# Two layers over an adjacency on one core: wo loaded by heads on SyncE, two weight rings, stores moved to SyncE and ScalarE, and the digits of a quarter of wq and wk made first and copied on chip

## The chip, the core and the metric

The kernel runs on one core of one Trainium2 chip. The time is the device time of one execution in microseconds (us). The kernel before was run three times: 2391.94, 2392.21 and 2393.85 us, median 2392.21 us.

## The reference

There are 64 graphs (batch entries) of 256 nodes with 512 features, x of shape 64 x 256 x 512 in float32, and one 0/1 matrix adj of 256 x 256 that all share. Layer 0 is masked attention with 8 heads of 64 columns, layer 1 multiplies by adj and by a weight; each adds its input and normalizes over the features.

```
q, k, v = x @ Wq + bq, x @ Wk + bk, x @ Wv + bv            # 8 heads of 64
scores  = q . k / 8 + (1 - adj) * -1e9
out     = softmax(scores) . v
x = layernorm(x + out @ Wo + bo)
x = layernorm(x + (adj @ x) @ weight + bias)
```

## The kernel before

The batch is worked in 32 pairs p (0 to 31) of two entries, so the four 128-row chunks of a pair make a moving operand of 512 columns.

**Digits.** A float32 product is made of three products of float32r operands. `split_high` (ScalarE, line 118), `split_rest` (VectorE, lines 123 and 124) and `split_scale` (ScalarE, line 127) cut a weight into the tiles high, low and diff; `x_high` and `x_rest` (lines 285, 289, 290) do it for x, `qk_high`, `qk_rest` and `k_low` (lines 378, 385 to 389, 394) for q and k. `product` (line 347) then issues 12 matmuls of 128 x 512 on line 339: three digits times four chunks k of the contraction, in the order low, high, diff of the second operand, or, for a few products marked `soon`, high first. Without digits a product takes four float32 matmuls.

**Weights.** The weights are cut once, in the first pairs, and each of the three digit tiles (1 MB) is kept in DRAM (`keep`, line 129, issued by GpSimd). From then on each stage loads its three tiles again (`load_w`, line 105, GpSimd). A stage is one of v, qk1 (heads 4 to 7 of q and k), o, qk0 (heads 0 to 3) and l; `STAGES` is their order, and a pool of six tiles `wr` holds the stage at work and the next one. `end_stage` starts the load of the stage after the next.

**Order.** PE, DVE (VectorE), ACT (ScalarE) and POOL (GpSimd) run in the order in which the program issues (`manual_schedule`); the queue of SP (SyncE), which loads and stores, is ordered by the framework. Each engine is in order: an instruction that waits holds all behind it.[...]

**The start.** `start` (line 696) writes the order of the first pair out by hand. Of q and k it multiplies the columns of heads 0 to 3 first: blocks (q, 0, 0), (k, 0, 0), (q, 0, 1), (k, 0, 1), each 128 columns of wq or wk, as float32, since no weight digits exist yet. Meanwhile DVE cuts x of pair 0 and then the weights of qk1 and v. Then follow `adj_t` (transposes of adj), `scores(0, 0)`, the blocks (q, 0, 2) to (k, 0, 3) and (v, 0, 0) to (v, 0, 3) with digits, `values(0, 0)` and `scores(0, 1)`. The digits of qk0, all 256 columns of wq and of wk, are cut in four steps (`ring_high`, `ring_rest`, `ring_scale` for k of 0 to 3) between v of pair 0 and `scores(0, 1)`; their first use is pair 1. `load_o` loads wo in four GpSimd DMAs, after which `bv_wo` multiplies bv by it.

**PSUM.** `banks` is a pool of eight banks. A score step takes eight at once, so the last score tiles wait until the tiles eight allocations earlier are copied out by ACT: in `values` those are zc (line 413) and vc (line 425).

**The end.** The last rows are normalized in two halves, one on ACT, one on DVE; ACT stores one (line 545), SP the other. A last check of the number range (line 782) lets every engine skip the general kernel behind it.

Of the kernel before, what the change touches and what calls it, by code (L numbers as in the profile page):

```python
# [15 lines left out]
P = 128  # L16
# [19 lines left out]
def fast(tc, x, adj, wq, bq, wk, bk, wv, bv, wo, bo, w1, b1, out):  # L36
# [34 lines left out]
    RAW, SCRATCH, W, UNCUT, BEGUN = {}, {}, {}, {}, {}  # L71

# [26 lines left out]
    STAGES += [("o", NP - 1), ("l", NP - 1)]  # L99
    ended = [0]  # L100

    def ring(name):
        return [wring.tile([P, 2, 2, D], F32R, name="wr") for _ in range(3)]

    def load_w(stage):
        name, p = stage
        if stage not in W and not (p in (0, NP - 1) and name in "ol"):
            W[stage] = ring(name)
            for i in range(3):
                nc.gpsimd.dma_start(W[stage][i], SCRATCH[name, i])  # L110

# [17 lines left out]
    def keep(name, i, part):  # L129

        SCRATCH[name, i] = scratch.tile([P, 2, 2, D], F32, name=f"{name}{i}")
        nc.gpsimd.dma_start(SCRATCH[name, i], part.bitcast(F32))

    def in_ring(f, name, p, k):

        stage = name, p
        if stage not in W:
            W[stage] = ring(name)
# [7 lines left out]
        if k == DC - 1 and f is not split_high:  # L146
            for i in (0, 2) if f is split_rest else (1,):
                keep(name, i, W[stage][i])

# [5 lines left out]

    def ring_scale(name, p, k):
        in_ring(split_scale, name, p, k)

# [38 lines left out]
    for i in range(4):  # L197
        load_x(1, i)
    bo_s, b1_s = on_all(bo, "bo"), on_all(b1, "b1")

    def small_ones():
# [6 lines left out]
    def load_o(k):  # L208
        if k % 2 == 0:
            RAW["o"] = two.tile([P, 2, D], F32, name="hl")  # L210
        RAW["o", k] = RAW["o"][:, k % 2]
        nc.gpsimd.dma_start(RAW["o", k], wo[k // 2 * HF:(k // 2 + 1) * HF].rearrange("(h a i) e -> a h i e", h=4, a=2)[k % 2])

    def load_l():
        t = two.tile([P, DC, D], F32, name="r")
# [58 lines left out]
    def x_t(p, k):  # L274
        if p < NP:
            XF[p, k] = two.tile([P, D], F32, name="xT")
            nc.vector.transpose(XF[p, k], XC.pop((p, k)))
            if p > 1 or k > 1:
                load_x(p + k // 2, (k + 2) % DC)

    def x_high(p, k):
# [32 lines left out]
    def operands(name, p, j, k):  # L314

        cols = slice(j * P, (j + 1) * P)
        if name == "v":
            pairs = [(XP[p, k][i][:, cols], W["v", p][i][:, k // 2, k % 2]) for i in range(3)]
        elif name in "qk":
            g, c = divmod(j, 2)  # L320
            if p == 0 and g == 0:
                return [(RAW[name][:, k, cols], XF[p, k])]
            e = slice(c * P, (c + 1) * P)
            w = [t[:, "qk".index(name)].rearrange("p s (k e) -> p (s k) e", k=2)[:, k, e] for t in W[f"qk{g}", p]]
# [6 lines left out]
        soon = p == 1 and name in "qk" and j == 0 or p == NP - 1 and name in "ol"  # L331
        return [pairs[i] for i in ((0, 1, 2) if soon else (1, 0, 2))]

    def parts_of(pm, name, p, j, of=(0, 3)):
# [12 lines left out]
    def product(name, p, j):  # L347
        if (name, p, j) in BEGUN:
            pm = BEGUN.pop((name, p, j))
            n = parts_of(pm, name, p, j, (1, 3))  # L350
        else:
            pm = banks.tile([P, D], F32, name="ps")
            n = parts_of(pm, name, p, j)
        scale = RHO if n == 3 else 1.0
        b, c = divmod(j, 2)
        if name in "ol":
            r = R[p][b][:, c]
            if c == 0:
                ST[p, name, b] = two.tile([P, 2], F32, name="sums")
            nc.vector.scalar_tensor_tensor(r, pm, scale, r, op0=OP.mult, op1=OP.add, accum_out=ST[p, name, b][:, c:c + 1])  # L360
        elif name == "v":
            if c == 0:
                V[p, b] = two.tile([P, NC, D], F32, name="v")
            nc.scalar.activation(V[p, b][:, c], pm, AF.Copy, scale=scale)
        else:
            T, bias = (K, bk_s) if name == "k" else (Q, bq_s)
            if c == 0:
                T[p, b] = one.tile([P, 2, 3, D], F32R if n == 3 else F32, name=name + "T")
            if n == 3:
# [326 lines left out]
    def start():  # L696
        make_identity(nc, ident)
        do(*((x_first, i) for i in range(4)), (biases,), *((x_high, 0, i) for i in range(4)), (small_ones,))
        qk1, v = (steps_of(*stage) for stage in STAGES[:2])
        high, rest, scale = ([(f, "qk0", 1, k) for k in range(DC)] for f in (ring_high, ring_rest, ring_scale))  # L700
        do((block, "q", 0, 0), (x_rest, 0, 0), (x_rest, 0, 1), qk1[0], (block, "k", 0, 0), (x_rest, 0, 2), (x_rest, 0, 3),
           qk1[1], (block, "q", 0, 1), qk1[2], v[0], (block, "k", 0, 1), v[1][:1], (x_t, 1, 0),
           (adj_t,), qk1[3])
        scores(0, 0)
        do(v[1][1:], (x_t, 1, 1), masks(0, 0, 0), (block, "q", 0, 2), v[2], *((load_o, k) for k in range(DC)), (qk_high, "q", 0, 2), (qk_rest, "q", 0, 2), v[3], (test_adj,),
           (block, "k", 0, 2), (x_high, 1, 0), (x_high, 1, 1), (qk_high, "k", 0, 2), (qk_rest, "k", 0, 2), masks(0, 0, 1),
           (block, "q", 0, 3), (k_low, 0, 2), (qk_high, "q", 0, 3), (qk_rest, "q", 0, 3), (x_rest, 1, 0), (x_t, 1, 2),
           (block, "k", 0, 3), (stage_end, 0), (qk_high, "k", 0, 3), (qk_rest, "k", 0, 3), (x_rest, 1, 1), (x_t, 1, 3), high[:2],
           (block, "v", 0, 0), (x_high, 1, 2), high[2:], (k_low, 0, 3), (block, "v", 0, 1), (x_rest, 1, 2),
           (block, "v", 0, 2), (x_high, 1, 3), (x_rest, 1, 3), (block, "v", 0, 3), (stage_end, 0), (load_r, 0), (load_l,))  # L710
        values(0, 0)
        scores(0, 1)
        do((bv_wo,), rest[:2], scale[:1], rest[2:3], scale[1:2], rest[3:], scale[2:])
        qk0 = [(f, name, 1, j) for j in range(2) for name in "qk" for f in (qk_high, qk_rest)]
        m = masks(0, 1, 0) + masks(0, 1, 1)
        do((begun, "q", 1, 0), (begun, "k", 1, 0), (block, "q", 1, 0), m[:4], qk0[:2], (block, "k", 1, 0), m[4:5], qk0[2:4], m[5:],
# [44 lines left out]
           (last_variance,), (root, 1), (less, p, "l", 1, c1), (normed, p, "l", 3, D // 2))  # L761

    PE, DVE, ACT, POOL = mybir.EngineType.PE, mybir.EngineType.DVE, mybir.EngineType.Activation, mybir.EngineType.Pool
    with tc.manual_schedule(engines={PE, DVE, ACT, POOL}):
        start()
        first(1, steps_of("o", 0))
# [2 lines left out]
        for w in range(2, NP - 1):  # L769
            first(w)  # L770
            second(w)
        ending()

    good = one.tile([P, 2, N // 32], F32, name="z")
# [186 lines left out]
```

## Time and profile before

| | |
|---|---|
| three runs, median | 2392.21 us (2391.94 to 2393.85) |
| the profiled execution | 2391.06 us, of which the span of the trace is 2389.2 us |
| PE busy | 2374.3 us, 99% of the span |
| DVE, ACT, POOL busy | 1991.0, 1505.4, 443.5 us |
| TensorE clock granted | 0.999 |
| DMA | 608.70 MB, 255 GB/s mean |

The sums below are made on the profiled span of 2389.2 us; the profiled execution took 1.9 us more than its span, and the median of the runs is 1.15 us above the profiled execution. In the profile's rows "idle before" is the idle time of the engine, and the arrow names what ended it. A DMA's "us to landing" runs from its issue on the queue to the arrival of its last byte.

### The profile page before, as it was taken

The numbers are of one execution on the slowest core, as the hardware profiler recorded it, in microseconds if no ns is written. First come the engines' busy times: TensorE is split into PE (matmuls) and PEld (weight loads), VectorE is DVE, ScalarE is ACT, GpSimd is POOL, SyncE is SP. The second block draws the span as 40 slices with busy tenths as digits, with TensorE's granted clock in tenths as the row PEclk, the third lists the DMA queues.
The fourth block names the chain that finished last, engine by engine and source line by source line (L and its number), as shares of the span: only waits on it lengthen the run. The fifth ranks groups of instructions, "written<-read, shape, count | busy, mean of one in ns | idle before, by whom it ended". The sixth has DMA issues, their size and how long they took to land.

```text
span 2389.2 us, 43002 instructions
## 1 busy us (share of the span) xinstructions
PE 2374.3 (99%) x16925; PEld 1907.5 (80%) x16925; DVE 1991.0 (83%) x3311; ACT 1505.4 (63%) x2793; POOL 443.5 (19%) x755
## 2 busy tenths in 40 slices
PE   9999999999999999999999999999999999999998
PEld 6788887888878888878888788887888878888776
DVE  7988888888888888888988888888888888888867
ACT  6666666566565665666656656666566665666655
POOL 1222111111111111121111112111111111121121
PEclk9999999999999999999999999999999999999999
DMA  9897788777888777887777967788778887777782
GB/s 295 274 310 244 265 255 283 259 230 256 260 265 271 241 237 256 264 293 238 236 255 254 310 240 224 265 255 286 258 227 261 261 264 268 238 244 255 256 274 62
DMA packets 373651, 608.70 MB, mean 255 GB/s; under 512 B 272316, under 2 KB 275908, under 8 KB 313156
## 3 DMA queue, kind: packets, MB, share of 16 engines
q0 software_dynamic: 71632, 500.21, 57.5%
q1 hardware_dynamic: 301104, 105.29, 20.4%
q8 instruction: 135, 2.21, 0.4%
q14 instruction: 72, 0.59, 0.1%
q10 hardware_dynamic: 708, 0.40, 0.1%
HBM read 551.29 MB, written 49.28 MB: 251 GB/s over the span
## 4 chain that ended last, share of the span: by engine, by line
PE 96%; DVE 1%; ACT 0%; issue 0%; POOLq 0%; ACTq 0%
PE ps L339 72%; PE ps L421 9%; PE ps L455 8%; PE ps L615 5%; PE ps L411 3%; DVE e L476 0%; DVE wr L124 0%; DVE wr L123 0%; PE ps L565 0%; DVE kT L389 0%; DVE qT L387 0%; DVE qT L385 0%; ACT kT L394 0%; DVE kT L385 0%; ACT waste L517 0%
## 5 line engine op out<-in xcount | busy, mean ns | idle before, releaser
L373 ACT ACTIVATE uncut<-ps,numbers 128x512 f32<-128x512 f32 x252 | 174.0, 690 | 274.0 <-PE ps L339 218.1
L476 DVE TENSOR_TENSOR e<-e,adjT 128x1024 f32<-128x1024 f32 x252 | 299.3, 1219 | 0.2 <-ACT e L470 0.2
L339 PE MATMUL ps<-low,wr 128*128 128x512 f32 x992 | 271.6, 395 | 0.0
L339 PE MATMUL ps<-wr,sl 128*128 128x512 f32 x1008 | 270.6, 390 | 0.1
L339 PE MATMUL ps<-wr,sh 128*128 128x512 f32 x1008 | 269.8, 389 | 0.0
L339 PE MATMUL ps<-wr,sd 128*128 128x512 f32 x1008 | 269.4, 389 | 0.0
L339 PE MATMUL ps<-high,wr 128*128 128x512 f32 x992 | 266.4, 390 | 0.0
L339 PE MATMUL ps<-diff,wr 128*128 128x512 f32 x992 | 265.0, 389 | 0.0
L523 POOL TENSOR_TENSOR ln<-ln,numbers 128x2 f32<-128x2 f32 x127 | 140.4, 1105 | 667.0 <-DVE ln L522 621.3
L470 ACT ACTIVATE e<-ps 128x512 f32<-128x512 f32 x504 | 253.3, 629 | 8.6 <-PE ps L455 8.6
L517 ACT ACTIVATE waste<-r,ln 128x512 bf16<-128x512 f32 x255 | 184.0, 722 | 104.6 <-DVE ln L510 98.9
L421 PE MATMUL ps<-e,v 128*32 128x256 f32 x4032 | 229.1, 379 | 0.0
L538 ACT ACTIVATE r<-r,ln 128x512 f32<-128x512 f32 x254 | 193.7, 811 | 55.1 <-DMA x<-in_x_dram 29.9
L339 PEld LDWEIGHTS ps<-wr,sh 128*128 128x128 f32 x1008 | 189.3, 188 | 39.9
L339 PEld LDWEIGHTS ps<-wr,sd 128*128 128x128 f32 x1008 | 189.2, 188 | 39.5 <-DMA wr<-o 0.2
L339 PEld LDWEIGHTS ps<-high,wr 128*128 128x128 f32 x992 | 186.2, 188 | 41.9 <-ACT e L470 0.8
L339 PEld LDWEIGHTS ps<-diff,wr 128*128 128x128 f32 x992 | 186.2, 188 | 39.1
L339 PEld LDWEIGHTS ps<-wr,sl 128*128 128x128 f32 x1008 | 186.9, 188 | 38.2 <-issue 0.4
L455 PEld LDWEIGHTS ps<-qT,kT 64*128 64x128 f32 x3056 | 187.8, 187 | 27.1 <-PE ps L421 12.4
L385 DVE SCALAR_TENSOR_TENSOR qT<-qT,uncut 128x512 fp32r<-128x512 f32 x126 | 86.8, 689 | 146.9 <-ACT qT L378 146.8
L339 PEld LDWEIGHTS ps<-low,wr 128*128 128x128 f32 x992 | 177.7, 188 | 35.5 <-ACT wr L127 0.6
L455 PE MATMUL ps<-qT,kT 64*128 64x256 f32 x3056 | 201.6, 285 | 0.5 <-ACT kT L394 0.5
(166 smaller groups left out, 4156.1 us busy)
## 6 DMA issues: line engine op xcount, KB each, us to landing
wr<-qk POOLq DMA_DIRECT2D x183, 1024.0 KB, 7.6
wr<-v POOLq DMA_DIRECT2D x93, 1024.0 KB, 6.8
wr<-o POOLq DMA_DIRECT2D x90, 1024.0 KB, 7.8
wr<-l POOLq DMA_DIRECT2D x90, 1024.0 KB, 8.6
r<-in_x_dram SPq DMA_DIRECT2D x32, 1024.0 KB, 12.0
out_dram<-r SPq DMA_DIRECT2D x62, 512.0 KB, 2.9
x<-in_x_dram SPq DMA_DIRECT2D x488, 64.0 KB, 5.4
qk<-wr POOLq DMA_DIRECT2D x6, 1024.0 KB, 8.3
```

Source lines behind the costliest of these rows:

```text
L339: nc.tensor.matmul(pm, *pairs[k][i], start=i == 0 and k == 0, stop=i == n - 1 and k == DC - 1)
L373: nc.scalar.activation(to, pm, AF.Identity, bias=bias[:, j:j + 1], scale=scale)
L385: nc.vector.scalar_tensor_tensor(low, high.bitcast(F32), -RHO, UNCUT.pop((name, p, j)), op0=OP.mult, op1=OP.add)
L411: nc.tensor.matmul(at[h * 32:(h + 1) * 32, b, :], ones, chunk[h], start=i == 0, stop=i == len(sm) - 1)
L421: nc.tensor.matmul(at[h * 32:(h + 1) * 32, a, :], V[p, b][:, kc, col:col + 32], E[p, g, b, kc][0][h % 2][:, h // 2, :], start=kc == 0, sto ...
L455: nc.tensor.matmul(sc[s][:, a, :], K[p, g][r, a, i, keys], Q[p, g][r, a, i, b * N:(b + 1) * N], start=i == digits[0], stop=i == digits[-1])
L470: nc.scalar.activation(e[s], sc[s], AF.Exp, scale=(RHO if (p, g) != (0, 0) else 1.0) * qscale)
L476: nc.vector.tensor_tensor(e, e, mask[:, kc:kc + 1, :].to_broadcast([P, e.shape[1], N]), op=OP.mult)
L517: nc.scalar.activation(waste, R[p][b][:, c], AF.Square, bias=t[0][:, c:c + 1], accum_out=t[1][:, c:c + 1])
L523: nc.gpsimd.tensor_tensor(t[2], t[1], power[:, cs], op=OP.pow)
L538: nc.scalar.activation(r[:, :cut], r[:, :cut], AF.Identity, scale=scale, bias=bias)
L615: nc.tensor.matmul(pm[:, j, :], t[:, i, mc, j * P:(j + 1) * P], adjT[:, mc, :], start=mc == 0 and i == 0, stop=mc == NC - 1 and i == 1)
```

## The change

- **Two rings.** The pool of six weight tiles becomes two pools of three, `wa` and `wb`, taken in turn by a stage's place in `STAGES`. The stage (v, 1) does not load its tiles again: it uses those of (v, 0), still in `wb`.
- **wo by heads.** Eight SP DMAs of 128 KB, four for each half of wo, in place of four GpSimd DMAs of 256 KB; they stand in SP's queue between the x loads of chunks 0, 1 and of chunks 2, 3 of pair 1.
- **Stores.** The digits of o and l are kept by SP instead of GpSimd. At the end both halves of the last rows are stored by ACT, and SP runs in program order as well.
- **The quarter.** The digits of the second 128 columns of wq and wk are cut first (`cut_high`, `cut_rest`, `cut_scale`), into tiles borrowed from the pools of low, diff, zc and vc. The blocks (q, 0, 1) and (k, 0, 1) use them: 12 matmuls each in place of four float32 ones. `cut_over` later copies them into the ring of (qk0, 1) by six SP DMAs of 256 KB; the first 128 columns are cut in place, in two steps each in place of four.
- The loads of x chunks 0 and 1 of pair 2 are issued after `cut_over`, before the loads of r and of the weight of layer 1.

```diff
-    wring = pool("wr", 6)
+    wrings = pool("wa", 3), pool("wb", 3)
...
+        if stage == ("v", 1):
+
+            W[stage] = W["v", 0]
+        elif stage not in W and not (p in (0, NP - 1) and name in "ol"):
+            W[stage] = ring(stage)
...
-        nc.gpsimd.dma_start(SCRATCH[name, i], part.bitcast(F32))
+        (nc.sync if name in "ol" else nc.gpsimd).dma_start(SCRATCH[name, i], part.bitcast(F32))
...
+        elif name == "qk0":
+
+            t = [w[:, k].rearrange("p s (k e) -> p (s k) e", k=2)[:, :, :P] for w in W[stage]]
+            f(RAW["qk"[k]][:, :, :P], t)
...
+    def cut(f, k):
+        if (k, 0) not in EARLY:
+            for i in range(3):
+                pool_of, name = ((four, "low"), (four, "diff"), (one, "zc"), (two, "vc"))[k + (2 if i == 2 else 0)]
+                EARLY[k, i] = pool_of.tile([P, DC, P], F32R, name=name)
+        f(RAW["qk"[k]][:, :, P:2 * P], [EARLY[k, i] for i in range(3)])
...
+    def cut_over():
+        W["qk0", 1] = ring(("qk0", 1))
+        for i, t in enumerate(W["qk0", 1]):
+            for k in range(2):
+                to = t[:, k].rearrange("p s (k e) -> p (s k) e", k=2)[:, :, P:2 * P]
+                nc.sync.dma_start(to.bitcast(F32), EARLY[k, i].bitcast(F32))
...
+        for h in range(4):
+            nc.sync.dma_start(t[h * 32:(h + 1) * 32], wo[g * HF + h * HD:g * HF + (h + 1) * HD].rearrange("(a i) e -> i a e", a=2))
...
-            if p == 0 and g == 0:
+            if p == 0 and j == 0:
                 return [(RAW[name][:, k, cols], XF[p, k])]
             e = slice(c * P, (c + 1) * P)
...
+            if p == 0 and g == 0:
+                w = [EARLY["qk".index(name), i][:, k] for i in range(3)]
...
-                    for queue, part in (nc.scalar, slice(0, cut)), (nc.sync, slice(cut, D)):
-                        if 0 < cut < D or part == slice(0, D):
-                            (queue if cut < D else nc.sync).dma_start(outr[p, b, :, c, part], r[:, part])
+                    for part in [slice(0, cut), slice(cut, D)] if 0 < cut < D else [slice(0, D)]:
+                        (nc.scalar if 0 < cut < D else nc.sync).dma_start(outr[p, b, :, c, part], r[:, part])
...
+        do((cut_high, 0), (cut_high, 1), (block, "q", 0, 0), (x_rest, 0, 0), (x_rest, 0, 1), (x_rest, 0, 2), (cut_rest, 0), (x_rest, 0, 3),
+           (cut_rest, 1), h, (cut_scale, 0), (block, "k", 0, 0), (cut_scale, 1), r[:2],
+           (block, "q", 0, 1), c[:2], r[2:], (block, "k", 0, 1), v[0], v[1][:1], (adj_t,), c[2:])
...
-           (block, "k", 0, 3), (stage_end, 0), (qk_high, "k", 0, 3), (qk_rest, "k", 0, 3), (x_rest, 1, 1), (x_t, 1, 3), high[:2],
+           (block, "k", 0, 3), (stage_end, 0), (cut_over,), (qk_high, "k", 0, 3), (qk_rest, "k", 0, 3), (x_rest, 1, 1), (x_t, 1, 3),
...
-        values(0, 0)
+        values(0, 0, (high[:1], high[1:]))
         scores(0, 1)
-        do((bv_wo,), rest[:2], scale[:1], rest[2:3], scale[1:2], rest[3:], scale[2:])
+        do(rest, scale, (bv_wo,))
```

From pair 1's scores to the end of the last pair but one, PE, DVE and ACT execute the same instructions in the same order in both kernels (two neighbours on DVE change places at the end).

More of the change, by code (lines that the diff above doesn't have):

```diff
@@ L70, in fast @@
     XC, XF, XP, R, Q, K, V, E, SM, O, SET, HL, ST, LN = ({} for _ in range(14))
-    RAW, SCRATCH, W, UNCUT, BEGUN = {}, {}, {}, {}, {}
+    RAW, SCRATCH, W, UNCUT, BEGUN, EARLY = {}, {}, {}, {}, {}, {}
     def load_x(p, i):
@@ L100, in fast, with ring @@
     ended = [0]
-    def ring(name):
-        return [wring.tile([P, 2, 2, D], F32R, name="wr") for _ in range(3)]
+    def ring(stage):
+        i = STAGES.index(stage) % 2
+        return [wrings[i].tile([P, 2, 2, D], F32R, name="w" + "ab"[i]) for _ in range(3)]
     def load_w(stage):
         name, p = stage
-        if stage not in W and not (p in (0, NP - 1) and name in "ol"):
-            W[stage] = ring(name)
+        if stage == ("v", 1):
+            W[stage] = W["v", 0]
+        elif stage not in W and not (p in (0, NP - 1) and name in "ol"):
+            W[stage] = ring(stage)
             for i in range(3):
@@ L137, in in_ring @@
         if stage not in W:
-            W[stage] = ring(name)
+            W[stage] = ring(stage)
         t = [w[:, k // 2, k % 2] for w in W[stage]]
@@ L145, in in_ring @@
             f(raw, [u.rearrange("p (k e) -> p k e", k=2) for u in t])
-        if k == DC - 1 and f is not split_high:
+        if k == (1 if name == "qk0" else DC - 1) and f is not split_high:
             for i in (0, 2) if f is split_rest else (1,):
@@ L157, in ring_scale, with cut_high, cut_rest, cut_scale @@
         in_ring(split_scale, name, p, k)
+    def cut(f, k):
[4 more added lines that the diff above has]
+        f(RAW["qk"[k]][:, :, P:2 * P], [EARLY[k, i] for i in range(3)])
+    def cut_high(k):
+        cut(split_high, k)
+    def cut_rest(k):
+        cut(split_rest, k)
+    def cut_scale(k):
+        cut(split_scale, k)
+    def cut_over():
[4 more added lines that the diff above has]
+                nc.sync.dma_start(to.bitcast(F32), EARLY[k, i].bitcast(F32))
     ones = cpool.tile([P, 32], F32, name="ones")
@@ L196, in fast @@
         nc.sync.dma_start(RAW["v", k], wv[k * P:(k + 1) * P])
-    for i in range(4):
+    for i in range(2):
+        load_x(1, i)
+    for g in range(2):
+        t = two.tile([P, 2, D], F32, name="hl")
+        for h in range(4):
+            nc.sync.dma_start(t[h * 32:(h + 1) * 32], wo[g * HF + h * HD:g * HF + (h + 1) * HD].rearrange("(a i) e -> i a e", a=2))
+        for a in range(2):
+            RAW["o", 2 * g + a] = t[:, a]
+    for i in range(2, 4):
         load_x(1, i)
@@ L206, in small_ones @@
             nc.gpsimd.memset(first_of_32[d * 32:d * 32 + 1], 1.0)
[L208 to L212, printed above, removed]
     def load_l():
@@ L277, in x_t @@
             nc.vector.transpose(XF[p, k], XC.pop((p, k)))
-            if p > 1 or k > 1:
+            if p > 1:
                 load_x(p + k // 2, (k + 2) % DC)
@@ L320, in operands @@
             g, c = divmod(j, 2)
-            if p == 0 and g == 0:
+            if p == 0 and j == 0:
                 return [(RAW[name][:, k, cols], XF[p, k])]
             e = slice(c * P, (c + 1) * P)
-            w = [t[:, "qk".index(name)].rearrange("p s (k e) -> p (s k) e", k=2)[:, k, e] for t in W[f"qk{g}", p]]
+            if p == 0 and g == 0:
+                w = [EARLY["qk".index(name), i][:, k] for i in range(3)]
+            else:
+                w = [t[:, "qk".index(name)].rearrange("p s (k e) -> p (s k) e", k=2)[:, k, e] for t in W[f"qk{g}", p]]
             pairs = [(w[i], XP[p, k][i]) for i in range(3)]
@@ L329, in operands @@
             pairs = [(t[i][:, k % 2, c * P:(c + 1) * P], W[name, min(p, NP - 2)][i][:, k // 2, k % 2]) for i in range(3)]
-        soon = p == 1 and name in "qk" and j == 0 or p == NP - 1 and name in "ol"
+        soon = name in "qk" and (p, j) in ((0, 1), (1, 0)) or p == NP - 1 and name in "ol"
         return [pairs[i] for i in ((0, 1, 2) if soon else (1, 0, 2))]
@@ L366, in product @@
             T, bias = (K, bk_s) if name == "k" else (Q, bq_s)
+            digits = (p, b) != (0, 0)
             if c == 0:
-                T[p, b] = one.tile([P, 2, 3, D], F32R if n == 3 else F32, name=name + "T")
-            if n == 3:
+                T[p, b] = one.tile([P, 2, 3, D], F32R if digits else F32, name=name + "T")
+            if digits:
                 to = UNCUT[name, p, j] = two.tile([P, D], F32, name="uncut")
@@ L698, in start @@
         do(*((x_first, i) for i in range(4)), (biases,), *((x_high, 0, i) for i in range(4)), (small_ones,))
[L699 to L703, printed above, removed]
+        h, r, c = ([(f, "qk1", 0, k) for k in range(DC)] for f in (ring_high, ring_rest, ring_scale))
@@ L704, in start @@
+        v = steps_of("v", 0)
+        high, rest, scale = ([(f, "qk0", 1, k) for k in range(2)] for f in (ring_high, ring_rest, ring_scale))
+        do((cut_high, 0), (cut_high, 1), (block, "q", 0, 0), (x_rest, 0, 0), (x_rest, 0, 1), (x_rest, 0, 2), (cut_rest, 0), (x_rest, 0, 3),
+           (cut_rest, 1), h, (cut_scale, 0), (block, "k", 0, 0), (cut_scale, 1), r[:2],
+           (block, "q", 0, 1), c[:2], r[2:], (block, "k", 0, 1), v[0], v[1][:1], (adj_t,), c[2:])
         scores(0, 0)
-        do(v[1][1:], (x_t, 1, 1), masks(0, 0, 0), (block, "q", 0, 2), v[2], *((load_o, k) for k in range(DC)), (qk_high, "q", 0, 2), (qk_rest, "q", 0, 2), v[3], (test_adj,),
+        do(v[1][1:2], masks(0, 0, 0), (x_t, 1, 0), v[1][2:], (x_t, 1, 1), (block, "q", 0, 2), v[2], (qk_high, "q", 0, 2), (qk_rest, "q", 0, 2), v[3], (test_adj,),
@@ L706, in start @@
            (block, "k", 0, 2), (x_high, 1, 0), (x_high, 1, 1), (qk_high, "k", 0, 2), (qk_rest, "k", 0, 2), masks(0, 0, 1),
            (block, "q", 0, 3), (k_low, 0, 2), (qk_high, "q", 0, 3), (qk_rest, "q", 0, 3), (x_rest, 1, 0), (x_t, 1, 2),
-           (block, "k", 0, 3), (stage_end, 0), (qk_high, "k", 0, 3), (qk_rest, "k", 0, 3), (x_rest, 1, 1), (x_t, 1, 3), high[:2],
-           (block, "v", 0, 0), (x_high, 1, 2), high[2:], (k_low, 0, 3), (block, "v", 0, 1), (x_rest, 1, 2),
-           (block, "v", 0, 2), (x_high, 1, 3), (x_rest, 1, 3), (block, "v", 0, 3), (stage_end, 0), (load_r, 0), (load_l,))
@@ L711, in start @@
-        values(0, 0)
+           (block, "k", 0, 3), (stage_end, 0), (cut_over,), (qk_high, "k", 0, 3), (qk_rest, "k", 0, 3), (x_rest, 1, 1), (x_t, 1, 3),
+           (block, "v", 0, 0), (x_high, 1, 2), (k_low, 0, 3), (block, "v", 0, 1), (x_rest, 1, 2),
+           (block, "v", 0, 2), (x_high, 1, 3), (x_rest, 1, 3), (block, "v", 0, 3), (stage_end, 0), (load_x, 2, 0), (load_x, 2, 1), (load_r, 0), (load_l,))
+        values(0, 0, (high[:1], high[1:]))
         scores(0, 1)
-        do((bv_wo,), rest[:2], scale[:1], rest[2:3], scale[1:2], rest[3:], scale[2:])
+        do(rest, scale, (bv_wo,))
@@ L763, in fast @@
     PE, DVE, ACT, POOL = mybir.EngineType.PE, mybir.EngineType.DVE, mybir.EngineType.Activation, mybir.EngineType.Pool
+    SP = mybir.EngineType.SP
     with tc.manual_schedule(engines={PE, DVE, ACT, POOL}):
@@ L771, in fast @@
             second(w)
+    with tc.manual_schedule(engines={PE, DVE, ACT, POOL, SP}):
         ending()
```

## The prediction

> **What bounds the kernel now.** I read the page first (PE busy 99%), then the table of stretches, to see where PE is not busy:
>
> ```profile
> 0.00:10.00 10.00, 5.65 (x22) 4.01 (x23) 2.70 (x7) 4.41 (x10) 1.20 (x13) 1.00 0.80 255
> 10.00:75.00 65.00, 64.54 (x441) 44.65 (x440) 59.44 (x86) 44.31 (x81) 11.53 (x21) 1.00 1.03 307
> 75.00:2300.00 2225.00, 2225.00 (x15917) 1795.06 (x15914) 1872.38 (x3088) 1407.24 (x2610) 414.68 (x698) 1.00 0.79 258
> 2300.00:2389.00 89.00, 79.12 (x555) 63.83 (x553) 56.52 (x133) 49.40 (x94) 16.05 (x23) 0.97 0.46 139
> ```
>
> After the stretch come its length, the busy time of PE, weight loads, DVE, ACT and POOL, the clock, the DMA share and GB/s. From 75 to 2300 us PE has no gap, and there the change leaves the order of PE, DVE and ACT as it is. So only what PE does up to about 75 us, and the tail, can move the time: the start shifts everything behind it by what it gains or loses. The second row also says that DVE (59.4 of 65 us) and the DMAs (share 1.03) are nearly full in that stretch; these two are the dangers. Next, PE's timeline of it:
>
> ```profile
> 8.18 14.00 PE L339 MATMUL ps<-e,r 128*128 128x512 f32 x32
> 22.01 0.60 PE L228 MATMUL ps<-z,vc 128*128 128x128 f32 x4
> 22.54 3.73 PE L455 MATMUL ps<-qT,kT 64*128 64x256 f32 x32
> 26.20 1.19 PE L339 MATMUL ps<-sl,wr 128*128 128x512 f32 x4
> ...
> 74.54 2.76 PE L455 MATMUL ps<-qT,kT 64*128 64x256 f32 x42 [0.46 <-ACT kT L394]
> ```
>
> The first row is the four float32 blocks; the last holds PE's only idle time between 8 and 2300 us that is worth a name, 0.46 us behind the digits of k of pair 1. The chain of waits gives the price of a block with digits:
>
> ```profile
> 77.30 32.86 PE ps L339 x144
> ```
>
> **The change, part by part.**
>
> *The two blocks.* Float32: (22.01 - 8.18) / 4 = 3.46 us a block. With digits: 12 x 32.86 / 144 = 2.74 us. Two blocks change: 2 x 0.72 = 1.44 us less PE work, all on the path, if their operands are there. Walking the new order with the old durations: DVE starts at 8.95 as before and needs 1.33 us for each pair of cuts. Three x_rest, cut_rest of q, the fourth x_rest and cut_rest of k end at 12.95, 14.28, 15.6 and 16.95 us; ACT's scale adds 0.6. PE, after two float32 blocks, wants (q, 0, 1) at 15.1, its low digits at 16.0, those of k at 18.8: all ready. The scores then start at 21.1, and (q, 0, 2) at 24.8 instead of 26.2. It needs the four cuts of qk1: DVE at 16.95 + 4 x 1.33 = 22.3, ACT at about 23.4. Cover 1.4 us. (v, 0, 0) at 35.7 needs the fourth cut of v: DVE is 1.3 us later than before by then (four more instructions, 2.7 us, less its hole of 1.39 us at 19.7), so 33.0, with ACT 33.6. Cover 2.1 us. The softmax sums are wanted at 46.7 and ready at about 41.4. So the early cuts cost nothing.
>
> *The first quarter later.* From 54 us DVE has four cuts of 0.67 us fewer (the other half of the eight), so it is 2.7 us freer just before the 0.46 us wait; its chain up to there was DVE without a hole. I take the wait as gone, 0.46 us; bounds 0 and 0.46.
>
> *The copies.* This is what the old trace does not show: six SP DMAs of 256 KB from SBUF to SBUF, in pieces of 512 bytes. They need PE's block (k, 0, 3) done (about 35.6 us)[...]. Behind them on SP stand the x, r and layer 1 weight loads, wanted from 75 us on. Waiting for copies 1 to 4 is x_rest of chunks 2 and 3 of pair 1, which gets its low and diff tiles from those that held the early digits (DVE, at 46.1 and 47.4 before); for copy 5 ACT's zc, for copy 6 ACT's second vc; behind DVE's wait stand the softmax normalization and the qk0 cuts, behind ACT's the exponentials of `scores(0, 1)`. POOL's qk0 store waits too, which covers itself: its reload is wanted at 87 us. ACT's timeline gives the places:
>
> ```profile
> 49.32 0.60 ACT L413 ACTIVATE zc<-ps 128x512 f32<-128x512 f32 x1 [0.43 <-PE ps L411]
> ...
> 52.77 0.60 ACT L425 ACTIVATE vc<-ps 128x512 f32<-128x512 f32 x1 [1.13 <-PE ps L421]
> 53.65 2.56 ACT L470 ACTIVATE e<-ps 128x512 f32<-128x512 f32 x5 [0.28 <-PE ps L455]
> ```
>
> With PE 1.4 us earlier: copy 5 is wanted at 47.9, copy 6 at 51.3. PE stands still only when it reaches the score banks that zc and vc free, at 52.6 and 53.4, or if the exponentials are so late that the masks and low digits behind them hold it. I put the point from which PE loses at 51.5 for copy 6, one for one after that.
>
> When do they land? [...] The DMA view of 30 to 50 us speaks against it:
>
> ```profile
> q0 software_dynamic: 1623, 5.00, 81.5%
> q1 hardware_dynamic: 3367, 0.91, 26.7%
> ...
> x<-in_x_dram SPq DMA_DIRECT2D x8, 64.0 KB, 15.0
> ```
>
> There SP's 64 KB loads took 15.0 us each beside POOL's queue. At that delay, the last copies, issued at about 41[...], would land at 56. Neither fits: the queue is an amount of work. Of POOL's share in this window, three loads of v (not all inside it) go away and wo moves ahead. I add up the DMA work due before the copies. POOL's: on the page, 500.21 MB in 57.5% of 2389.2 us, 2.88 us per 1 MB tile; six stores of qk1 and v are 17.3. SP's, at the packet times of the trace (92 ns for 2 KB, 16 ns for the 128 bytes of x, over 16 engines): 4.25 MB of first loads 12.8, sixteen x loads 8.2, wo 3.0, two biases 1.5. Sum 42.8 us, at a share of 1.05 from 2 us on: done at about 43. The six copies at the 28 ns of the trace's 512-byte packets are 0.9 us each, 5.4 in all: 48, and with 2 us to land copy 2 is in at 46.3, copy 4 at 48.1, copy 6 at 49.9. That is 1.6 us before the point, with a DVE wait of a few tenths that its holes of 1.20 and 0.84 us at 49 and 52.6 take up. Ends: 0 if they land by 51.5; +4.5 us if the last lands at 56. I take 0.2, nearer the sum than the row, since the sum counts what is queued, but the margin is thin.
>
> *wo on SP.* Eight DMAs ahead of x chunks 2 and 3: 3 us more before those. They landed at 32 us and are wanted at 42.2 and 45.5; now about 42 by the sum above, wanted at 41 to 44 us. This is the same thin margin, counted there. wo itself is wanted at 55.
>
> *Two rings, no reload of (v, 1).* Ring order and so the waits for free tiles are the same; 3 MB, 8.6 us of DMA, go away between 37 and 60 us. PE did not wait for it (landed before 60, wanted at 77): 0.
>
> *Stores of o and l on SP.* They wait for their digits at about 90 and 120 us; behind them stand x loads of pair 3, issued at 104.7 before and wanted near 150, and r of pair 1, wanted near 155. 0.
>
> *The last stores.* SP issued its half at 2381.75 and the row before it at 2382.12, ACT its own at 2381.94; now ACT issues both, the second some 0.4 us later, and SP's row goes about 1 us earlier. SP's last landing is at 2385.4, and POOL's closing instruction ends at 2388.1 whatever lands: 0, bounds -0.4 and +0.4.
>
> Sum: -1.44 - 0.46 + 0.2 = -1.7 us; allowing 0.1 for small shifts, span 2389.2 to 2387.6. The profiled execution would be 2389.5, and the median of the runs, 1.15 us above it as before, 2390.6.
>
> **The rivals.**
>
> 1. *The copies come late* (slower). One mechanism: SP's copies share the DMA engines with POOL's stores of v and stand behind wo and x; DVE, then ACT, then PE's score banks wait. For it: the 15.0 us row. Against it: 3 MB fewer. From 51.5 us on each us costs one; from 53.4 the kernel is slower than before. At 56: -1.9 + 4.5 = +2.6, 2394.8. To be slower by 4.8 us the last would have to land after 58.
> 2. *The gain is eaten by DVE* (no change). The early cuts make DVE late by 1.3 us while PE comes 1.4 early; if another order of waits on ACT (the scales of v stand ahead of the copy-out of (k, 0, 2)) adds two us, PE waits at `scores(0, 0)` or (v, 0, 0) for what it gained: 2392.2. Against it: covers of 1.4 and 2.1 us.
> 3. *PE is not what ends* at the tail: the stores cost their upper bound of 0.4 and the 0.46 us wait stays: -1.44 + 0.4, so 2391.2.
>
> **Numbers.** My forecast (copies in time, -1.2 to -2.3): 0.66, around 2390.6, own range 2389.9 to 2391.3. Rival 1: 0.20, 2391.3 to 2397, centre 2394.8. Rival 2: 0.08. Rival 3: 0.06. About 0.2% (4.8 us) is what a measurement of this kernel can tell from no change. Faster by that: PE's work alone leaves 2387 at best, 0.01. Slower by it: only the far end of rival 1, 0.05. Within: 0.94. The range, with the 1 us spread of the runs, 2389.6 to 2394.2, leaves half of rival 1 and a little below out.
>
> **What would show it.** Right: no `e,r` row beyond two blocks (x16 in 6.9 us); 24 matmuls on low, diff, zc, vc from 15.1 us; PE's `sl` row at 24.8; (v, 0, 0) at 35.7; copies landing by 51; no idle PE near 53 or 72; PE 1.9 us earlier at 100 us, and the tail as long as before. Wrong: idle PE on L495 near 53 us released by ACT or DVE behind a copy or an x load (rival 1); idle PE at 21 to 37 us (rival 2); a tail from PE's end to the span's end above 10 us (rival 3).

## The result, and the profile after

| | before | changed |
|---|---|---|
| median of 19 runs each | 2391.76 us (2391.0 to 2393.85) | 2387.89 us (2386.96 to 2390.18) |
| ratio, 95% interval | | 0.9984 [0.9978, 0.999] |
| profiled execution, its span | 2391.06, 2389.2 | 2387.83, 2386.1 |
| PE's end to the span's end | 10.0 | 7.9 |

The change takes 3.9 us off, where I had forecast 1.6 (2390.6 against 2392.2) and a range that ended at 2389.6. First the table of stretches of the changed kernel, with the columns that the prediction explained:

```profile
0.00:10.00 10.00, 5.45 (x19) 4.00 (x20) 2.24 (x6) 3.91 (x9) 1.20 (x13) 1.00 0.77 240
10.00:75.00 65.00, 65.00 (x467) 47.93 (x467) 61.88 (x91) 46.53 (x85) 7.12 (x14) 1.00 0.93 294
```

PE has no idle time left between 10 and 75 us (65.00; it was 64.54), DVE is fuller (61.9 of 65 us) and the DMA share fell from 1.03 to 0.93 (the 3 MB of v are not loaded again). PE's timeline answers to the one of before row by row:

```profile
8.67 7.59 PE L378 MATMUL ps<-e,r 128*128 128x512 f32 x16 [0.27 <-ACT e L301]
15.70 1.49 PE L378 MATMUL ps<-sh,low 128*128 128x512 f32 x4
...
21.61 0.60 PE L264 MATMUL ps<-z,vc 128*128 128x128 f32 x4
22.14 4.10 PE L495 MATMUL ps<-qT,kT 64*128 64x256 f32 x32
26.17 1.20 PE L378 MATMUL ps<-sl,wa 128*128 128x512 f32 x4
...
73.13 3.14 PE L495 MATMUL ps<-qT,kT 64*128 64x256 f32 x48
76.20 1.19 PE L378 MATMUL ps<-wb,low 128*128 128x512 f32 x4
```

Two float32 blocks are left, the blocks with digits follow, and the row at 73.13 has no wait in brackets any more. But PE is only 0.03 us earlier at 26.17, and 1.03 at 76.20. So of the 3.1 us by which the two spans differ, PE brings 1.1 and the tail 2.05. Cut into stretches, from the start times of the same instructions in both traces:

| stretch of PE | before | changed | difference |
|---|---|---|---|
| span's start to the second float32 matmul step | 8.71 | 9.66 | +0.95 |
| from there to the transposes of adj (the four blocks) | 13.30 | 11.95 | -1.35 |
| to block (q, 0, 2) (`scores(0, 0)`) | 4.19 | 4.56 | +0.37 |
| to the scores of pair 1, heads 0 to 3 | 47.25 | 46.96 | -0.29 |
| to the next scores (holds the wait of 0.46) | 41.10 | 40.39 | -0.71 |
| to PE's last matmul | 2264.68 | 2264.63 | -0.05 |
| PE's last matmul to the span's end | 9.96 | 7.91 | -2.05 |

Three rows are not in my sum: +0.95, +0.37 and -2.05. The last one is the largest. The rows of the program's closing line show it (engine's queue, operation, count, then shortest, median and longest in ns), here of the kernel before:

```profile
L956 POOLq DRAIN  x3: 46/107/6479, 2381.6 to 2388.9; - x3
```

and of the changed one:

```profile
L998 POOLq DRAIN  x3: 40/107/4524, 2380.5 to 2385.8; - x3
```

GpSimd's closing drain (the longest of the three DRAIN instructions in these rows) takes 4.52 us in place of 6.48. I had seen it in the trace of before, and had taken its end for fixed.

### The profile page after: what moved, and what is told of

It reads as the page before. It is cut to its first block, busy times and chain, and to the rows that moved or that the text cites. A ratio compares the mean times of both kernels' runs of the same rounds, so it can differ in the third digit from the quotient of the medians.

```text
span 2386.1 us, 43032 instructions
## 1 busy us (share of the span) xinstructions
PE 2373.5 (99%) x16933; PEld 1909.6 (80%) x16933; DVE 1989.9 (83%) x3311; ACT 1502.5 (63%) x2793; POOL 434.0 (18%) x742
## 4 chain that ended last, share of the span: by engine, by line
PE 99%; DMA 0%; ACT 0%; DVE 0%; issue 0%; POOLq 0%; SPq 0%; ACTq 0%
PE ps L378 74%; PE ps L461 9%; PE ps L495 8%; PE ps L654 5%; PE ps L451 3%; DMA low<-in_x_dram 0%; PE ps L297 0%; PE ps L604 0%; ACT waste L557 0%; PE ps L277 0%; PE ps L284 0%; DVE r L606 0%; DVE r L399 0%; ACT waste L612 0%; ACT r L578 0%
## 5 line engine op out<-in xcount | busy, mean ns | idle before, releaser
L461 PEld LDWEIGHTS ps<-e,v 128*32 128x32 f32 x4032 | 131.0, 110 | 86.5
L399 DVE SCALAR_TENSOR_TENSOR r<-ps,r 128x512 f32<-128x512 f32 x255 | 174.7, 685 | 23.3 <-PE ps L378 21.2
L524 DVE TENSOR_TENSOR sm<-e,e 128x1024 f32<-128x1024 f32 x126 | 154.1, 1223 | 3.2
L654 PEld LDWEIGHTS ps<-adjT,hl 128*128 128x128 f32 x1024 | 138.0, 189 | 9.5
L425 DVE SCALAR_TENSOR_TENSOR kT<-kT,uncut 128x512 fp32r<-128x512 f32 x126 | 86.7, 688 | 67.4 <-ACT kT L418 67.4
L654 PE MATMUL ps<-adjT,hl 128*128 128x256 f32 x1024 | 141.0, 281 | 0.0
L378 PE MATMUL ps<-low,wa 128*128 128x512 f32 x512 | 140.2, 395 | 0.0
L378 PE MATMUL ps<-wb,sl 128*128 128x512 f32 x512 | 137.5, 390 | 0.1
L378 PE MATMUL ps<-high,wa 128*128 128x512 f32 x512 | 137.5, 390 | 0.0
L378 PE MATMUL ps<-wb,sh 128*128 128x512 f32 x512 | 137.0, 389 | 0.0
```

The lines of the kernel that those rows point to most:

```text
L378: nc.tensor.matmul(pm, *pairs[k][i], start=i == 0 and k == 0, stop=i == n - 1 and k == DC - 1)
L425: nc.vector.scalar_tensor_tensor(low, high.bitcast(F32), -RHO, UNCUT.pop((name, p, j)), op0=OP.mult, op1=OP.add)
L461: nc.tensor.matmul(at[h * 32:(h + 1) * 32, a, :], V[p, b][:, kc, col:col + 32], E[p, g, b, kc][0][h % 2][:, h // 2, :], start=kc == 0, sto ...
L524: nc.vector.tensor_tensor(t, e0, e1, op=OP.add)
L654: nc.tensor.matmul(pm[:, j, :], t[:, i, mc, j * P:(j + 1) * P], adjT[:, mc, :], start=mc == 0 and i == 0, stop=mc == NC - 1 and i == 1)
```

## The experiments

In "tail" below I mean PE's last matmul to the span's end, from each kernel's own trace (the first expectations count it from the start of the last matmul, 10.2 and 8.1 us). All medians stand beside runs of the kernel before on the same chip.

**Is it the new end?** Four kernels: the new end alone, all but the new end, SP's order alone, and all but the quarter.

```diff
 # new end alone: the kernel before, with
+                    for part in [slice(0, cut), slice(cut, D)] if 0 < cut < D else [slice(0, D)]:
+                        (nc.scalar if 0 < cut < D else nc.sync).dma_start(outr[p, b, :, c, part], r[:, part])
...
+    with tc.manual_schedule(engines={PE, DVE, ACT, POOL, SP}):
         ending()
```

> The kernel before, with nothing but the new end: both halves of the last rows stored by ACT, SP in program order, so that SP's full row goes ahead of what waits for DVE. Theory T (in the traces PE's end to the span's end fell from 10.2 to 8.1 us, and that is the end's own doing): 2.0 us less than the kernel before, tail 8.1 us, and GpSimd's closing instruction about 4.5 us instead of 6.5. Rival S (the shorter tail is chance or follows from something in the start, as the prediction's 0 for the stores would have it): 0, tail 10.2 us.

Measured: 2391.74 us, ratio 1.0001 [0.9993, 1.0009], tail 9.95 us. The drain is as before:

```profile
L957 POOLq DRAIN  x3: 46/107/6479, 2382.1 to 2389.4; - x3
```

My theory fell. SP had issued its last store earlier than before and ACT its own later, and the end of the program moved with neither.

The changed kernel with these lines taken back:

> The changed kernel with the old end (SP stores the DVE half, and the framework orders SP's queue). Theory T: only the start's gain is left, 1.1 us by the traces (PE ends 1.1 us earlier), and 1.9 us by the medians (3.9 less 2.0), with a tail of about 10.2 us. Rival S: all of the gain, 3.9 us less than the kernel before.

Measured: 2387.91 us, 0.9984 [0.9977, 0.9991], tail 8.10 us, and the short drain. All of the gain is there without the new end.

```profile
L997 POOLq DRAIN  x3: 40/107/4524, 2381.9 to 2387.4; - x3
```

```diff
 # SP's order alone: the kernel before, with
+    with tc.manual_schedule(engines={PE, DVE, ACT, POOL, SP}):
         ending()
```

> The kernel before, with only SP in program order in the last pair: SP's full row goes out first and the half from DVE last, still on SP. If the early row is what shortens the tail (its 256 KB out of the way): 1 to 2 us less than the kernel before. If it is that SP is done early and leaves for the end (its own last issue no longer waits for DVE): nothing, within 0.4 us, and a tail of about 10 us. Rival S: 0.

Measured: 2391.54 us, 1.0 [0.9992, 1.0008], tail 9.96 us: nothing.

```diff
 # no quarter: the changed kernel, with start() of the kernel before (without load_o), and
-            if p == 0 and j == 0:
+            if p == 0 and g == 0:
                 return [(RAW[name][:, k, cols], XF[p, k])]
...
-            if p > 1:
+            if p > 1 or k > 1:
                 load_x(p + k // 2, (k + 2) % DC)
```

> The changed kernel without its early quarter: the order of the start and the four float32 blocks as in the kernel before, but two rings, no reload of v for pair 1, wo by heads on SP, stores of o and l on SP, and the new end. The start by the prediction's step: two float32 blocks more cost 1.44 us, and the wait of 0.46 us at 74.5 us is back: slower than the changed kernel by 1.1 us (as the traces show) to 1.9 (as predicted), so 2.0 to 2.8 us less than the kernel before. If the start's gain came from the lighter DMA load instead (3 MB of v not reloaded): as fast as the changed kernel, and no wait at 74.5 us.

Measured: 2390.02 us, 0.9994 [0.9986, 1.0003], tail 7.92 us. So the quarter is worth 2.1 us by the medians (2390.02 to 2387.9), near the 1.9 of the prediction and not the 1.1 that the first pair of traces showed. The intervals of the two ratios overlap, so the 2.1 is rough. What is left of the change is 1.7 us below the kernel before by the medians, with an interval that just holds no change; that the tail is worth its 2.05 us rests on the traces. Its PE timeline has the four float32 blocks and the wait back:

```profile
8.57 14.84 PE L372 MATMUL ps<-e,r 128*128 128x512 f32 x32 [0.27 <-ACT e L297]
...
75.78 2.42 PE L489 MATMUL ps<-qT,kT 64*128 64x256 f32 x36 [0.46 <-ACT kT L428]
```

And the short tail comes with what is left in this kernel: rings, no reload of v, wo by heads, stores on SP.

**Is it the length of GpSimd's program?** In all kernels with the short tail GpSimd's program has 18 or 20 instructions fewer, and packets of instructions are fetched while it drains. (Four begin in the drain of the trace of before, three of 8 KB and one of 16 KB, and as many in that of the changed kernel; the last of 8 KB comes behind that of 16 KB before, and ahead of it in the changed one.)

```diff
 # 30 memsets more: the kernel before, with, at the end of small_ones
+        spare = cpool.tile([P, 1], F32, name="spare")
+        for i in range(30):
+            nc.gpsimd.memset(spare, float(i))
```

> The kernel before with 30 more one-column memsets on GpSimd in its first microseconds, where GpSimd is idle; nothing else moves. The new end did not shorten the tail (9.95 us with it alone), but every kernel whose GpSimd program is some 18 instructions shorter (1353 or 1351 in place of 1371) has a tail of 7.9 to 8.1 us, and one instruction packet of 8 KB fewer before GpSimd's closing instruction ends. Theory L (where GpSimd's closing instructions lie in its program against the 8 KB pieces in which it is fetched): moved on by 29 they lie in one piece too, so 2.0 us less than the kernel before, tail near 8.0 us, and no packet of 8 KB between the second of 16 KB and the end of GpSimd's closing instruction. Rival N (the other parts of the change shorten the tail: fewer GpSimd DMAs, stores on SP, or another engine's program): 0, tail 9.95 us.

Measured: tail 9.97 us, and the drain to the ns as before:

```profile
L959 POOLq DRAIN  x3: 50/107/6479, 2382.8 to 2389.9; - x3
```

The median, 2390.81 us (0.9996 [0.9988, 1.0004]), is 0.9 below that of the kernel before, and its interval holds no change.

The same in the changed kernel, with 19:

> The changed kernel with 19 one-column memsets more on GpSimd in its first microseconds, so that GpSimd's program has 1371 instructions as in the kernel before. Theory L: 2.0 us more than the changed kernel, so about 1.9 us less than the kernel before, tail back at 10 us. Rival N: as the changed kernel, 3.9 us less than the kernel before.

Measured: 2387.28 us, 0.9982 [0.9975, 0.9989], tail 8.23, drain 4524 ns. The program's length has no part in the drain's. What stayed was that the drain has exactly two lengths in ten traces, and that the short one goes with fewer DMAs on GpSimd.

**Which DMAs?** One move at a time, each in the kernel before.

```diff
 # stores on SP
-        nc.gpsimd.dma_start(SCRATCH[name, i], part.bitcast(F32))
+        (nc.sync if name in "ol" else nc.gpsimd).dma_start(SCRATCH[name, i], part.bitcast(F32))
```

> The kernel before with the six stores of the digits of o and l moved from GpSimd to SP, nothing else. The closing drain of GpSimd takes one of two times in the ten traces, whatever runs ahead of it: 6.47 us in the kernel before, with the new end, with SP's order and with 30 memsets more, 4.53 us in every kernel that has all of the change's moves away from GpSimd's DMA queue. So it is not the length of its program; the claim left is theory D: the drain depends on what GpSimd's queue of DMAs did. If these six stores (2 us each as other traffic, long done) are what counts: drain 4.5 us, tail near 8 us, 2 us less than the kernel before. If the wo loads, the reload of v or a sum of all count: 6.47 us, tail 9.96 us, as the kernel before.

```profile
L956 POOLq DRAIN  x3: 46/107/5989, 2382.3 to 2388.9; - x3
```

```diff
 # wo on SP
+        for h in range(4):
+            nc.sync.dma_start(t[h * 32:(h + 1) * 32], wo[g * HF + h * HD:g * HF + (h + 1) * HD].rearrange("(a i) e -> i a e", a=2))
...
-        nc.gpsimd.dma_start(RAW["o", k], wo[k // 2 * HF:(k // 2 + 1) * HF].rearrange("(h a i) e -> a h i e", h=4, a=2)[k % 2])
```

> The kernel before with wo loaded by heads in eight SP DMAs in place of four GpSimd DMAs of 256 KB, nothing else. Theory D with wo as the cause (of GpSimd's DMAs these four alone have a pattern in four dimensions with rows of one head): drain 4.5 us, tail near 8 us, 2 us less than the kernel before. Otherwise 6.47 us and 9.96 us. In the start I expect no effect, within 0.3 us.

```profile
L959 POOLq DRAIN  x3: 40/107/5259, 2381.9 to 2387.7; - x3
```

```diff
 # two rings, no reload
+        if stage == ("v", 1):
+            W[stage] = W["v", 0]
```

> The kernel before with two rings of three tiles and no reload of v for pair 1 (three GpSimd DMAs of 1 MB fewer), nothing else. Theory D with the number of DMAs or of their bytes as the cause, reached by three fewer: drain 4.5 us, tail near 8 us, 2 us less than the kernel before. Otherwise 6.47 us and 9.96 us. The wait of 0.46 us at 74.5 us stays, since DVE has as much to do ahead of it.

```profile
L960 POOLq DRAIN  x3: 46/107/6234, 2384.1 to 2390.9; - x3
```

Each expectation named two values, and each run gave a third between them. The medians (2391.16, 2389.98 and 2392.08 us; 0.9998 [0.9989, 1.0006], 0.999 [0.9982, 0.9999], 0.9999 [0.9991, 1.0008]) could not have told this; the drain does: 490 ns for six stores, 1220 ns for four wo loads, 245 ns for three loads of v. The sum is 1955 ns, and 6479 - 4524 is 1955. An ordinary DMA counts 81.7 ns, one of the wo loads, which gather 32 rows from each of four heads, 305; what makes these dearer no run shows. All of these stand in the first 125 us of the program, so it was open whether DMAs elsewhere count too.

```diff
 # 13 DMAs more: the changed kernel, with, in the loop over pairs
+            if 5 <= w < 18:
+                nc.gpsimd.dma_start(spare, mask)
```

> The changed kernel with 13 more GpSimd DMAs (256 KB each, the constant adjacency tile to a spare place in DRAM, one in each of pairs 5 to 17; nothing reads them). The closing drain so far: 6.47 us in the kernel before, 5.99 with six stores fewer on GpSimd (0.08 each), 6.23 with three loads fewer (0.08 each), 5.25 with the four wo loads fewer (0.305 each), 4.53 with all of these fewer; 0.48 + 0.24 + 1.22 = 1.94, which is the whole difference. Theory C (the drain counts every GpSimd DMA, wherever it stands in the program): 4.53 + 13 x 0.08 = 5.57 us, and the tail 0.8 to 1.0 us longer than the changed kernel's 7.9. Theory F (only the DMAs of the first pairs count, since all that were taken away stand there): 4.53 us and 7.9.

```profile
L1001 POOLq DRAIN  x3: 40/107/5586, 2382.8 to 2388.9; - x3
```

```diff
 # 12 DMAs fewer: the kernel before, with
+                if name == "qk1" and 10 <= p < 14:
+                    nc.sync.dma_start(W[stage][i].bitcast(F32), SCRATCH[name, i])
+                else:
                     nc.gpsimd.dma_start(W[stage][i], SCRATCH[name, i])
```

> The kernel before with twelve of its 1 MB weight loads (qk1 of pairs 10 to 13) issued by SP in place of GpSimd. Theory C: drain 6.47 - 12 x 0.08 = 5.51 us, tail 9.0. Theory F: 6.47 us and 9.96. In the middle PE may wait for an x load that now stands behind a weight load on SP; what it costs there shows as idle PE before 2300 us and has nothing to do with the drain.

```profile
L959 POOLq DRAIN  x3: 46/107/5499, 2382.7 to 2388.7; - x3
```

5586 - 4524 is 1062, 13 x 81.7; 6479 - 5499 is 980, 12 x 81.7. Theory C holds to the ns where it was tried: a DMA of 256 KB added in pairs 5 to 17 and one of 1 MB taken away in pairs 10 to 13 change GpSimd's closing drain by the same 0.08 us as those of the first 125 us. Medians: 2390.11 us (0.9994 [0.9986, 1.0003]) and 2391.19 us (0.9999 [0.999, 1.0008]), tails 8.75 and 8.69. The medians do not show the drain's part alone: both traces have idle PE between 2091 and 2095 us as well (1.4 and 0.5 us), whose cause is not known, and the first kernel is 2.2 us slower than the changed one where its drain makes 1.1. So the price of a DMA is read from the drains in the traces. What stays open is why the other 470 DMAs do not show: at 81.7 ns each they would make 38 us, and the drain is 4.5.

**The start: PE's clock.** The row +0.95 of the table is no wait. In the kernel before the last transposes of x run at 0.11 us each, from 7.3 us on; in the changed one they take 0.21 to the end, and the first float32 step 0.99 in place of 0.53. The same instructions take either time in the traces of both starts: PE's steps halve at 7.3 us (before), about 9.6 (changed), and in the changed kernel with the old end only at 12.7, where the two float32 blocks took 9.19 us:

```profile
8.57 9.19 PE L378 MATMUL ps<-e,r 128*128 128x512 f32 x16 [0.17 <-ACT e L301]
```

The profile's table of stretches prints a granted clock of 1.00 here, but only because it takes time without a record for full speed: the trace's first record of the granted clock, at 1.00, begins at 7.28, 9.62 and 12.75 us in these three traces, just where the steps halve. So PE's first microseconds run at half the later speed (0.21 us a transpose in place of 0.11), and the trace has no clock for them. Over the nine traces with the start of before, this first record begins between 7.28 and 11.73 us, over the six with the changed start and no work put ahead of it between 7.26 and 12.75: when it comes differs between executions, and the change is not shown to move it. I tried to bring it forward.

```diff
 # small matmuls first: the changed kernel, with, at the head of start()
+        pt = banks.tile([P, D], F32, name="ps")
+        for i in range(24):
+            nc.tensor.matmul(pt[0:32, 0:32], ones, ones, start=True, stop=True)
```

> The changed kernel with 24 small matmuls on PE (32x32 ones, results not used) while it waits for the first x, from about 1 us. In the six traces so far PE's first instructions run at half speed (a 128x128 transpose 0.21 us, a float32 matmul step 0.85 in place of 0.43) and double their speed at a point that differs from run to run, from 7.3 us (before) over 9.6 (after) to 12.7 (the changed kernel with the old end). If that point follows PE's first work, it comes up to 3 us earlier here: the transposes end at 7.2 instead of 8.2, no slow float32 step is left, and the kernel takes 1 to 1.5 us less than the changed one in the median (4.9 to 5.4 less than before). If it does not follow, or if the first x alone sets the start: 0.

Measured: 2387.84 us, 0.9982 [0.9974, 0.9989]. PE did the small matmuls from 0.9 to 3.7 us, and the record of the full clock began at 10.36 us all the same. A miss.

**The start: DVE at `scores(0, 0)`.** The row +0.37 is one: DVE copies the transposed adj out of its PSUM bank behind the first two cuts of v, and the eighth score tile takes this bank.

```profile
24.39 0.68 DVE L265 CAST adjT<-ps 128x512 fp32r<-128x512 f32 x1
```

In the kernel before it was done at 23.68, in the changed one at 25.07.

```diff
 # adj copy ahead: the changed kernel, with
-           (block, "q", 0, 1), c[:2], r[2:], (block, "k", 0, 1), v[0], v[1][:1], (adj_t,), c[2:])
+           (block, "q", 0, 1), c[:2], r[2:], (block, "k", 0, 1), v[0], (adj_t,), c[2:], v[1][:1])
```

> The changed kernel with the copy of the transposed adj ahead of the second cut of v on DVE. In the changed kernel that copy ends at 25.07 us and the last score bank of scores(0,0) waits for it (matmuls at 25.05 and 25.11 in place of a pair at 24.84); before, it ended at 23.68, ahead of need. If PE loses 0.3 us there, this is 0.3 us faster than the changed kernel (scores(0,0) 3.66 us long again instead of 4.03), less than the medians can tell, but seen in the trace. If the wait only moves on to the cut of v that is now later, nothing: the row of (v,0,0) at 37.2 us stays where it is against scores(0,0).

Measured: 2387.47 us, 0.9983 [0.9977, 0.999]. The row of `scores(0, 0)` has its old length again, and (q, 0, 2) follows after 3.65 us; the median cannot tell the 0.4 us from none:

```profile
21.25 3.72 PE L495 MATMUL ps<-qT,kT 64*128 64x256 f32 x32
24.90 1.20 PE L378 MATMUL ps<-sl,wa 128*128 128x512 f32 x4
```

The next step takes both: the copy ahead, and transposes of full width in place of small matmuls.

```diff
 # full transposes first: the kernel above, with, at the head of start()
+        pt = banks.tile([P, DC, P], F32, name="ps")
+        for i in range(12):
+            nc.tensor.transpose(pt[:, i % DC, :], ident, ident)
```

> The changed kernel with the copy of adj ahead on DVE and 12 transposes of the 128x128 identity on PE (results not used) from 1.4 us to the first x at 3.9. The 24 small matmuls of 32x32 before this did not bring the doubling of PE's speed forward (it came at about 10.2 us). [...] If transposes of full width count as busy and 32x32 ones do not:[...] transposes or float32 steps at half speed gone, and 0.5 to 1 us less than with the copy of adj alone (2387.5). If it is [...]work on x alone that counts: as with the copy of adj alone, with a doubling anywhere from 7.3 to 12.7 us.

Measured: 2386.80 us, 0.9978 [0.997, 0.9986]. It is the fastest kernel of the study, 5.2 us below the kernel before and by the medians 1.1 below the changed one (the two intervals overlap).

```profile
1.43 2.82 PE L738 MATMUL ps<-z 128*128 128x128 f32 x12 [1.43 <-POOL z masks.py:199]
...
8.18 0.20 PE L307 MATMUL ps<-z 12*128 12x12 f32 x1 [0.69 <-DMA z<-in_L_gnn_bv_dram]
8.31 7.13 PE L378 MATMUL ps<-e,r 128*128 128x512 f32 x16
```

The transposes of x fall from 0.21 to 0.11 us each at 5.7 us, where the record of the full clock begins (5.75), the earliest of all traces, and no float32 step is slow. What begins the blocks at 8.31 is now the small bias load (0.69 us of idle PE behind it). It is one trace: that full-width work is what brought it forward is not shown. The runs fit an early full clock: 13 of the 14 lie between 2386.28 and 2387.05 us, where those of the changed kernel spread from 2386.96 to 2390.18.

**The copies, put late.** This is the prediction's rival 1, made to happen.

```diff
 # copies late: the changed kernel, with, ahead of the copies in cut_over()
+        for i in range(2):
+            nc.sync.dma_start(spare, W["qk1", 0][i].bitcast(F32))
```

> The changed kernel with two stores of 1 MB (a weight tile to a spare place in DRAM; nothing reads them) put on SP among the copies of the quarter, so that the copies land 5.8 us later by the 2.9 us of a 1 MB tile: about 55.7 in place of 49.9. The prediction's rival 1 puts the point from which PE loses at 51.5, one for one: 4.2 us more than the changed kernel, an idle PE near 53 us on the scores' banks, and by the trace's 1.1 us of room in place of 1.6 perhaps more. If the copies' consumers (x_rest of pair 1, zc, vc) have more room than the prediction gave them: 0 to 2 us more.

Measured: 2394.80 us, 1.001 [1.0004, 1.0017], 6.9 us more than the changed kernel. The fifth copy landed at 57.2 us, where in the changed kernel the sixth was in at 49.9. PE's timeline has the idle time where rival 1 put it, released by ACT's zc and vc:

```profile
53.00 1.81 PE L498 MATMUL ps<-qT,kT 64*128 64x256 f32 x25
57.90 1.58 PE L498 MATMUL ps<-qT,kT 64*128 64x256 f32 x12 [3.08 <-ACT zc L456]
59.91 1.65 PE L498 MATMUL ps<-qT,kT 64*128 64x256 f32 x11 [0.43 <-ACT vc L468]
```

and ACT's says what held zc:

```profile
57.25 0.60 ACT L456 ACTIVATE zc<-ps 128x512 f32<-128x512 f32 x1 [7.03 <-DMA wa<-zc]
```

ACT did nothing else in these 7.03 us: the cut of `wa` that follows zc (L122) ran at 57.74 us, in the changed kernel at 50.21.

From these scores' first matmul to pair 1's scores PE takes 27.63 us in place of 20.51: 7.1 lost. Of these 3.5 are the idle time. The rest is mostly PE's clock, which the profile shows at half from 58.32 to 65.15 us, just behind the idle time (the row's columns are those of the prediction's table):

```profile
58.32:65.15 6.83, 6.40 (x33) 3.92 (x30) 6.59 (x11) 6.83 (x15) 1.62 (x5) 0.50 0.87 237
```

The same eight matmuls, here and in the changed kernel:

```profile
61.49 1.94 PE L280 MATMUL ps<-hl,numbers 128*32 128x512 f32 x8
...
55.69 1.06 PE L277 MATMUL ps<-hl,numbers 128*32 128x512 f32 x8
```

6.40 us of work at half clock lose 3.2 us; 3.5 and 3.2 are 6.7 of the 7.1, and from 66.12 us on PE loses nothing more. So rival 1's mechanism and place are right, and the idle time is what its price of one for one speaks of; the half clock, nearly as much again, was in no one's sum. As an estimate from this trace (57.2 less the 3.5 of idle time), PE starts to lose at 53.7 us, 53.3 on the changed kernel's clock, whose scores begin 0.38 earlier. The prediction's 51.5 was walked for a PE that reaches (q, 0, 2) at 24.8; the changed kernel reached it at 26.17, which makes it 52.9.

## Why the prediction was wrong

**The step that failed** is the tail, in the words of the prediction: "SP's last landing is at 2385.4, and POOL's closing instruction ends at 2388.1 whatever lands: 0, bounds -0.4 and +0.4." The half about landings is right: the new end alone gave 1.0001 and the same tail. The other half took the instruction's length for a constant. It changes with the DMAs that GpSimd issues, 0.08 us for each and 0.3 for a wo load, and the change takes 13 away. So the zeros at "two rings, no reload of (v, 1)" and "stores of o and l on SP", and the tail that "wo on SP" did not cost at all, were wrong by 0.25, 0.49 and 1.22 us: 1.96 of the 2.05. (Two small terms nearly cancel beside it: a pause of 0.3 us behind the drain is gone, and SP's own closing work now ends 0.24 us after the drain, so in this trace a still shorter drain would gain nothing.) I had costed these three moves where they were made, in the first 125 us. There 0 fits: with each move alone PE has the one wait near 75 us as before (0.48, 0.49 and 0.45 us) and no other.

**The two blocks**: -1.44 forecast, -1.35 measured. DVE's cuts came as walked (next instructions at 13.44, 14.76, 16.09 and 17.42 us, each 0.47 to 0.49 later than forecast, as DVE began 0.49 later).

**The wait of 0.46 us**: gone as forecast, and back without the quarter.

**The copies**: landed at 45.9 (first), 47.4 (third) and 49.9 (sixth); forecast 46.3 for the second, 48.1 for the fourth, 49.9 for the sixth. They were issued from 39.5 (first) to 45.2 us (sixth). (The forecast's 2 us to land is, in the trace of before, the shortest of all stores of the result, 2.0 us; their median is 2.9.) Adding up the queued work was right to a few tenths, where the 15.0 us row would have given 56. (Its 12.8 us for 4.25 MB of first loads should be 12.5 at 92 ns for 2 KB, which changes little.) No engine waited for a copy. The margin was not 1.6 us but some 3, by the estimate of 53.3 that the late copies give.

**Rival 2** happened in a place that my walk had left out: the copy of adj as the release of a score bank. It cost 0.37 us.

**(q, 0, 2) at 24.8, (v, 0, 0) at 35.7, PE 1.9 us earlier at 100 us**: 26.17, 37.20 and 1.0. These miss by the +0.95 of PE's slow first steps, which lasted 2.3 us longer in this execution than in that of before, and by the 0.37. Without the +0.95, PE is 2.0 us earlier, and the quarter's worth by medians is 2.1. So the forecast of the start, -1.7, was about right, and the sum of start and tail, -2.0 - 2.05, is near what the medians show: -3.9.

## What to carry to other kernels

A closing instruction that waits for nothing visible is still a term of the sum: ask what its length depends on before putting it at a constant, and cost an operation that is removed where it stood and at the program's end. Two single traces of this start differ by a microsecond in the first ten because PE comes to its full speed at another time in each (7.28 and 9.62 us); anchor stretches at the same instruction behind that, and let an experiment's median say what the start is worth. Idle PE cost more than the idle time where the copies were late: 3.1 us of it were followed by 6.8 us at half clock. When a wait's cover is worked out, list every tile whose release PE needs there: the copy of adj stood in no data path of the scores, only in their bank.

## What the runs showed of the hardware

- GpSimd's closing drain: 6479 ns in the kernel before and 4524 in the changed one, the same to the ns in every kernel with the same GpSimd DMAs (four traces with 6479, eight with 4524). A DMA more or less, 256 KB in pairs 5 to 17, 1 MB in pairs 10 to 13 or in the first 125 us: 81.7 ns; a wo load (256 KB, rows gathered from four heads): 305 ns.
- PE's steps are twice as long at first (transpose 0.21 us against 0.11, float32 step of 512 columns 0.85 against 0.43), and the point where they halve lies between 7.3 and 12.7 us in traces whose first transposes start at 3.7 to 4.0, 3.5 to 8.9 us behind these. 2.8 us of 32x32 matmuls ahead left it at 10.4 us in one trace, 2.8 us of 128x128 transposes ahead went with 5.7 us in another. The trace's record of the granted clock begins, at 1.00, at these points; time before it has no record and is printed as 1.00.
- With the copies late, 3.1 us of idle PE were followed by a granted clock of 0.50 for 6.83 us, and PE's steps took twice as long there too (eight matmuls 1.94 us in place of 1.06).
